# Graph attention layer on one core: who copies h in the node stage, the spacing of that stage's steps, and where the later chunks' indices stand

## The chip, the cores and the metric

The kernel runs on 1 core of one Trainium2 chip. The metric is device microseconds of one execution, lower is better. The kernel before takes 5714.75 us in the median of 3 runs (5710.31 to 5733.31).

## What is computed

One graph attention layer with a residual, over 12,500 nodes of 128 features and 412,500 edges sorted by their target:

```python
h  = relu(layernorm(x))                                   # 12500 x 128
hh, q, k, v = h @ Wn + bn, h @ Wq + bq, h @ Wk + bk, h @ Wv + bv
eh = edge_features @ We + be                              # 412500 x 128
hmid   = leaky_relu(concat(q[src], k[tgt], eh) @ A1 + b1, 0.2)
scores = leaky_relu(hmid @ A2 + b2, 0.2)                  # 8 heads
w   = softmax(scores.mean(-1), axis=0)                    # over all edges
out = segment_sum(w[:, None] * v[tgt], src)
y   = hh + out
x + gamma * (y - mean(y)) / sqrt(var(y) + eps) + beta
```

The edges arrive sorted by target, and the sum goes by source, so every edge has to be moved once.

## The kernel before

**Tiles and chunks.** Nodes are padded to 98 tiles of 128, edges to 403 groups of 8 tiles. The groups are cut into 11 chunks; the first has 57 groups (456 tiles), the next three 43 each. Each chunk goes through two stages.

**First stage** (`first_stage`). A step makes two edge tiles: four matmuls fill one PSUM bank with key and value parts (L1007 from the edge features, L1010 from a window of the node table `kv_tab`, picked by a one-hot matrix that VectorE makes at L984). One step later ScalarE copies the bank to a ring of 20 rows (L994, and L991 for the row's place), and GpSimd scatters the two tiles by indirect DMA to their sources' blocks in a table in HBM (L924). A group is four such steps, so chunk 0 has 228 of them.

**Second stage** (`second_stage`). It reads a chunk's part of the table back (L1038), computes scores and weights, and adds weighted values per node. It can begin with a chunk only when that chunk's scatters have landed.

**What must stand beside chunk 0.** In chunk 0 no second stage runs yet. Four other jobs are laid among its first-stage steps:

- `nodes` computes the node tables. A block of 4 node tiles takes 28 steps; 25 blocks follow one another, each in a software pipeline. Layer norm: `centre` (L673 to L675, VectorE), `square` (L680, ScalarE), `spread` (L685 and L687, VectorE), `root` (L690, ScalarE), `scale` (L695 and L696, VectorE). Then `turn` transposes on TensorE (L702) and `relu` evicts (L707, ScalarE). Per node tile `project` makes h, q, k and v in one PSUM bank `mp` (L714, L716). h is copied out by `keep_h` (L719). The other three are split into three bfloat16 parts, so that bfloat16 matmuls keep their precision: `upper` rounds (L722, ScalarE), `lower` subtracts (L726, VectorE), `middle` rounds the rest (L729, ScalarE), `lowest` subtracts again (L732, VectorE). `store` issues seven DMAs per block: three of `kv_tab` on SyncE's queue (L738), one of `hn_tab` (L741) and three of `q_tab` (L743) on ScalarE's queue.
- `ready(0)` and `ready(1)` give every edge of chunks 0 and 1 its slot in the table ("numbering"): a one-hot matrix on VectorE (L572), two matmuls (L579), a maximum on VectorE (L635), and after every 40 tiles a row of small VectorE operations (L593 to L619).
- `index(k)` turns the raw indices of chunk k into places, blocks and window offsets: two loads on SyncE's queue (L354, L355), thirteen VectorE operations (L359 to L392), a matmul (L371) and transposes (L398), ScalarE copies (L403, L407) and DMAs on ScalarE's queue (L381, L404, L408).
- `clear_ends` writes zeros to the table's ends (L232, SyncE).

**What sets the order.** Each engine runs its instructions in the order in which they were written out here. `interleave` deals out one step at a time of the job that is furthest behind in its share, so jobs are mixed evenly and end together. `nodes` instead is drawn by a rule inside `first_stage`: about 3.2 of its steps for each step of the first stage. Inside `nodes`, `at(t, order, job)` writes each job into a table of steps; the number is the step, counted from the block's own start t or from a node tile's start u = t + 7j. In the interleave of chunk 0 the index and numbering work is one single chain: `index(1)`, then all of `ready(1)`, then `index(2)` to `index(10)`.

Where two engines read one PSUM bank, the recording layer puts the one behind the other: `keep_h` on VectorE waits for `upper` on ScalarE, since both read `mp`.

Of the kernel before, what the change touches and what calls it, by code (L numbers as in the profile page):

```python
# [16 lines left out]
AF = mybir.ActivationFunctionType  # L17
# [48 lines left out]
NB = 4  # L66
# [3 lines left out]
LEAD = 4  # L70
# [5 lines left out]
def _ceil(a, b):  # L76
    return -(-a // b)


def interleave(*jobs):  # L80

    jobs = [[g, max(n, 1), 0] for g, n in jobs]
    while jobs:
        job = min(jobs, key=lambda j: (j[2] + 0.5) / j[1])
        try:
            next(job[0])
            job[2] += 1
        except StopIteration:
            jobs.remove(job)


def some_steps(job, n):
# [29 lines left out]
def kernel(ctx: ExitStack, tc: tile.TileContext, n_edges, x, src, dst, ea, w_nv, w_qt, w_kt,  # L122
# [12 lines left out]
    nc = tc.nc  # L135
    NP = x.shape[0]
    NTN = NP // P
# [13 lines left out]
    NC = len(chunks)  # L151
# [259 lines left out]
    def index_steps(c):  # L411
        return 12 + 2 * _ceil(chunks[c][1] * SUPER, QUAD * P)
# [228 lines left out]
    def ready(c):  # L641

        yield from count(c)
        yield from plan(c)
        yield from place_slots(c)

    def ready_steps(c):
        nt = chunks[c][1] * SUPER
        return _ceil(nt, (8 if c == 0 else 5) * STR) + 4 + 2 * _ceil(nt, STR)
# [10 lines left out]
    def nodes():  # L660
# [55 lines left out]
            nc.tensor.matmul(flat, lhsT=once3, rhs=bias3, start=False, stop=True, skip_group_check=True)  # L716

        def keep_h(b, j):
            nc.vector.tensor_copy(hns[b][:, j, :], mp[b, j][:, 0, :])  # L719

        def upper(b, j):
            nc.scalar.activation(partss[b][:, j, 0, :], mp[b, j][:, 1:4, :].rearrange("p a d -> p (a d)"), AF.Copy)  # L722
# [25 lines left out]
        def at(t, order, job, *args):  # L748
            when.setdefault(t, []).append((order, len(when.get(t, ())), job, args))

        for b in size:

            t = 28 * b
            at(t - 52, 9, load, b)
            for k, job in enumerate((centre, square, spread, root, scale)):
                at(t - 16 + 2 * k, 8, job, b)
            at(t - 5, 0, turn, b)
            at(t - 3, 0, relu, b)
            for j in range(size[b]):
                u = t + 7 * j  # L760
                at(u, 3, project, b, j)
                at(u + 3, 4, upper, b, j)
                at(u + 4, 5, keep_h, b, j)
                at(u + 5, 5, lower, b, j)
                at(u + 7, 4, middle, b, j)
                at(u + 9, 5, lowest, b, j)
            at(t + 35, 7, store, b)
        for t in range(min(when), max(when) + 1):
            for _, _, job, args in sorted(when.get(t, []), key=lambda j: j[:2]):
                job(*args)  # L770
            yield

    stored = [0]
    node_at = [0, 28 * _ceil(NTN, NB) + 35 - 2 * LEAD]


    acc = ctx.enter_context(tc.tile_pool(name="acc", bufs=1)).tile([P, NTN, D], FP, name="acc")
# [490 lines left out]
    for i, w in enumerate(units):  # L1268
        t = 2 * w["start"] - (19 if w["nq"] > 2 else 17)
# [143 lines left out]
    for c in range(NC + 1):  # L1413
        jobs = []
        if c == NC:
            count_left()
        elif c == 0:
            with tc.manual_schedule(engines={ET.PE, ET.DVE, ET.Activation, ET.SP}):
                next(first)
        if c < NC:  # L1420
            jobs.append((some_steps(first, chunks[c][1] * halves + (c == NC - 1)), chunks[c][1] * halves))
        if c > 0:
            n = ends[c] - ends[c - 1]
            idle = LEAD if c == 1 else 0
            if c == NC:
                jobs.append((fetch_early(), early + 2))
            jobs.append((chain(some_steps(second, n - 8), any_left(), some_steps(second, 8)) if c == NC else
                         chain(iter([None] * idle), some_steps(second, n - idle)), n))
        if c == 0:
            jobs.append((first_ready, (ready_steps(0) - ready_enough()) * 6 // 5))  # L1430
            jobs.append((chain(index(1), ready(1), *(index(k) for k in range(2, NC))),
                         ready_steps(1) + sum(index_steps(k) for k in range(1, NC))))
        elif c + 1 < NC:
            jobs.append((ready(c + 1), ready_steps(c + 1)))
        if c == 0:
            jobs.append((chain(*(clear_ends(k) for k in range(1, TABS))), (TABS - 1) * NTN))
        if c == 0:
            with tc.manual_schedule(engines={ET.PE, ET.DVE, ET.Activation, ET.SP}):
                interleave(*jobs)
                for _ in node_steps:  # L1440
                    pass
            setup.close()
            pb = main.enter_context(tc.tile_pool(name="pb", bufs=1))
            ps = main.enter_context(tc.tile_pool(name="ps", bufs=5))
            pq = main.enter_context(tc.tile_pool(name="pq", bufs=4))
            pw = main.enter_context(tc.tile_pool(name="pw", bufs=8))
            p3 = main.enter_context(tc.tile_pool(name="p3", bufs=1))
            ps_h = main.enter_context(tc.tile_pool(name="ps_h", bufs=2, space=PSUM))
            ps_s = main.enter_context(tc.tile_pool(name="ps_s", bufs=1, space=PSUM))
            ps_o = main.enter_context(tc.tile_pool(name="ps_o", bufs=1, space=PSUM))  # L1450
        else:
            with tc.manual_schedule(engines={ET.PE, ET.DVE, ET.Activation, ET.SP}):
                interleave(*jobs)
        if c < TABS:
            clear_holes(c)
# [90 lines left out]
```

## Time and profile before

| what | value |
|---|---|
| median of 3 runs | 5714.75 us |
| the profiled execution: its own time | 5704.97 us |
| its span, first to last instruction | 5703.2 us |
| TensorE / VectorE / ScalarE / GpSimd busy over the span | 77% / 71% / 33% / 57% |
| granted TensorE clock, mean | 0.879 |
| chunk 0: first scatter starts, last scatter ends | 72.1 us, 811.2 us |
| `keep_h`: copies, mean each | 98, 286 ns |

The span of the profiled execution is 1.8 us under its time, and its time 9.8 us under the median of the runs. PE is TensorE, DVE VectorE, ACT ScalarE, POOL GpSimd, SP SyncE; PEld is a weight load, and a q behind an engine's name is its sequencer. In a row of a group stand line, engine, operation, output and input, the count, then busy time in us and the mean of one in ns, then the engine's idle time just ahead of it and what ended it.

### The profile page before, as it was taken

What the parts mean: (1) busy time and instruction counts of PE and PEld (TensorE: products, weight loads), DVE (VectorE), ACT (ScalarE), POOL (GpSimd) and SP (SyncE); (2) the same over time, 40 slices, a digit from 0 to 9 for tenths busy, and PEclk for the clock granted to TensorE, in tenths of its full rate; (3) what the DMA queues carried; (4) which work ended last, traced back from release to release, by engine and by line L of the source; (5) the groups of instructions that cost most, each with busy time, mean ns of one, the idle gap of its engine ahead of it and who ended that gap; (6) DMA issues with size and microseconds to landing.
All of it is one profiled execution on the core that took longest, in us unless ns stands there. A gap on an engine that the chain in (4) does not pass through costs nothing. (4 is left out here: it accounts for less than half of the span.)

```text
span 5703.2 us, 86990 instructions
## 1 busy us (share of the span) xinstructions
PE 4378.4 (77%) x26559; PEld 3030.7 (53%) x26559; DVE 4076.2 (71%) x12996; ACT 1897.7 (33%) x5104; POOL 3239.9 (57%) x3250
## 2 busy tenths in 40 slices
PE   6766647877777777777777877778777787778898
PEld 3333324555555555555555555555555555556674
DVE  7777526776777666667776767777777776667898
ACT  2333322333333333333333333333333333333346
POOL 3666566665566555665655655665655665665510
PEclk8888768998898888888888988888989888989999
DMA  4667767777777777776777767777776776778985
GB/s 134 202 196 218 212 208 226 243 246 224 226 241 234 224 225 241 236 234 222 239 227 232 244 224 239 231 242 232 245 236 215 247 237 210 253 236 273 304 280 198
DMA packets 711378, 1316.75 MB, mean 231 GB/s; under 512 B 152208, under 2 KB 362309, under 8 KB 710889
## 3 DMA queue, kind: packets, MB, share of 16 engines
q1 hardware_dynamic: 492080, 867.97, 52.1%
q0 software_dynamic: 154704, 424.26, 20.1%
q10 hardware_dynamic: 64105, 18.76, 1.4%
q8 instruction: 214, 3.51, 0.3%
q14 instruction: 275, 2.25, 0.1%
HBM read 820.50 MB, written 490.10 MB: 230 GB/s over the span
## 5 line engine op out<-in xcount | busy, mean ns | idle before, releaser
L924 POOL DMA_INDIRECT tab<-row,slots x3223 | 3236.7, 1004 | 2211.9 <-ACT row L994 979.8
L1192 PE MATMUL o_ps<-rows_of,w 128*128 128x128 f32 x6860 | 1020.7, 292 | 313.4 <-DVE w L1179 170.0
L1192 PEld LDWEIGHTS o_ps<-rows_of,w 128*128 128x128 f32 x6860 | 913.5, 201 | 440.3 <-issue 258.8
L994 ACT ACTIVATE row<-row_ps 128x512 f32<-128x512 f32 x1151 | 681.2, 593 | 1126.1 <-PE row_ps L1010 343.4
L1102 ACT ACTIVATE low<-h_ps 128x512 f32<-128x512 f32 (+1 forms) x861 | 511.8, 594 | 1438.6 <-remote 432.6
L1007 PE MATMUL row_ps<-w_ea,ea_t 128*128 128x256 f32 x2302 | 821.6, 442 | 188.0 <-ACT row L994 127.0
L1179 DVE TENSOR_SCALAR w<-iota_f,rows_of,score 128x128 f32<-128x128 f32 x3381 | 954.6, 357 | 0.1
L1103 DVE TENSOR_TENSOR rows_of<-h_ps,low 128x512 f32<-128x512 f32 (+1 forms) x861 | 589.1, 684 | 497.5 <-ACT low L1102 335.0
L1093 PE MATMUL h_ps<-sel_q,qw 128*128 128x128 fp8e4 (+3 forms) x4242 | 766.9, 314 | 5.4 <-issue 5.2
L1007 PEld LDWEIGHTS row_ps<-w_ea,ea_t 128*128 128x128 f32 x2302 | 425.8, 214 | 420.9 <-issue 186.3
L1110 PE MATMUL s_ps<-rows_of,a_sb 128*32 128x384 f32 (+2 forms) x2392 | 314.7, 604 | 384.4 <-DVE rows_of L1103 257.2
L1088 PE MATMUL h_ps<-ident,rows_of 128*128 128x128 f32 x3430 | 580.1, 295 | 5.8 <-issue 5.8
L1010 PEld LDWEIGHTS <-sel 126*128 126x128 fp8e4 x3224 | 344.2, 107 | 298.4 <-issue 77.7
L1088 PEld LDWEIGHTS h_ps<-ident,rows_of 128*128 128x128 f32 x3430 | 455.1, 154 | 83.0 <-issue 44.4
L1010 PE MATMUL row_ps<-kv,sel 126*128 126x256 bf16 x2302 | 489.1, 296 | 7.0 <-issue 4.6
L1093 PEld LDWEIGHTS <-qw 128*128 128x128 bf16 x4242 | 412.5, 104 | 134.7 <-issue 39.8
L635 DVE TENSOR_REDUCE num<-run 128x5 f32<-128x490 f32 (+1 forms) x648 | 425.9, 657 | 6.4 <-PE run L579 2.2
L994 ACT ACTIVATE row<-t_bank 128x512 f32<-128x512 f32 x461 | 273.5, 593 | 465.9 <-PE t_bank L1010 190.6
L579 PE MATMUL run<-one,rest_b 128*128 128x500 f16 x637 | 263.1, 413 | 210.8 <-DVE num L635 127.9
L984 DVE TENSOR_SCALAR sel<-offs,third 126x512 fp8e4<-126x512 uint8 x806 | 365.4, 494 | 64.9 <-remote 31.8
L1078 DVE TENSOR_SCALAR sel_q<-pls,part 128x512 fp8e4<-128x512 uint8 (+1 forms) x837 | 367.7, 492 | 0.0
L1148 DVE TENSOR_SCALAR_CACHE_REDUCE s_ps<-s_ps,less_of 128x128 f32<-128x128 f32 x298 | 105.9, 355 | 365.6 <-PE o_ps L1192 114.7
(249 smaller groups left out, 4420.3 us busy)
## 6 DMA issues: line engine op xcount, KB each, us to landing
rows_of<-tab SPq DMA_DIRECT2D x264, 1542.0 KB
ea_t<-in_ea SPq DMA_DIRECT2D x403, 256.0 KB
qw<-q_tab SPq DMA_DIRECT2D x192, 384.0 KB
tab<-row,slots POOLq DMA_INDIRECT x3223
offs<-off_d SPq DMA_DIRECT2D x403, 126.0 KB
pls<-pl_d SPq DMA_DIRECT2D x264, 192.0 KB
rows_of<-tab SPq DMA_DIRECT2D x27, 1028.0 KB
qw<-q_tab SPq DMA_DIRECT2D x96, 288.0 KB
```

The lines of the kernel that those rows point to most:

```text
L635: nc.vector.tensor_reduce(num, strips[:, :NTN, :m].rearrange("p b m -> p m b"), AX.X, ALU.max)
L924: i = nc.gpsimd.indirect_dma_start(out=tab[:, :], out_offset=bass.IndirectOffsetOnAxis(ap=slots[c][t // (8 * STR)][:m, t % (8 * STR):t % ( ...
L994: nc.scalar.activation(row[:, :, 1:ROW], bank, AF.Copy)
L1007: nc.tensor.matmul(bank[:, :, 0:D], lhsT=ea_g[:, ts(k, P)], rhs=w_ea, start=True, stop=False, skip_group_check=True)
L1010: nc.tensor.matmul(bank[:, b, :], lhsT=sel[:, ts(b * halves + k, P)], rhs=kv, start=False, stop=True, skip_group_check=True)
L1078: nc.vector.tensor_scalar(sel[:, a:b], plss[i][:, a:b], part1, None, op0=ALU.is_equal, saturate=False)
L1088: nc.tensor.matmul(h_ps[:, ts(j, P)], lhsT=rows_of[i][:, a + j, 1:D + 1], rhs=ident, is_transpose=True, start=j == 0, stop=False, skip_gro ...
L1093: nc.tensor.matmul(h_ps[:, (x0 - a) * P:(x1 - a) * P], lhsT=qws[i][:, s, ts(k, D)], rhs=plss[i][:, x0 * P:x1 * P], start=False, stop=k == ...
L1102: nc.scalar.activation(low, h_ps, AF.Copy, scale=SLOPE)
L1103: nc.vector.tensor_max(rows_of[i][:, a:b, 1:D + 1], h_ps.rearrange("p (j e) -> p j e", j=m), low.rearrange("p (j e) -> p j e", j=m))
L1179: nc.vector.tensor_scalar(w, iota_f, rows_of[i][:, t, 0:1], state["score", i][:, t:t + 1], op0=ALU.is_equal, op1=ALU.mult)
L1192: nc.tensor.matmul(state["o_ps"][:, ts(t // ct, D)], lhsT=w, rhs=rows_of[i][:, t, D + 1:ROW], start=t == 0, stop=t % ct == ct - 1, skip_gr ...
```

## The change

Three things:

1. `keep_h` is an ACTIVATE on ScalarE instead of a copy on VectorE.
2. Inside `nodes` the distances grow. Layer norm: `centre` starts 20 steps ahead of the block instead of 16, and the links then stand 2, 3, 4 and 3 steps apart instead of 2 each; `scale` stays 8 ahead. Split: `keep_h` stays at u+4, `lower` goes from u+5 to u+6, `middle` from u+7 to u+10, `lowest` from u+9 to u+13. `store` goes from t+35 to t+36.
3. `index(2)` to `index(10)` no longer follow `ready(1)`; a new `mixed` (the body of `interleave` as a generator) deals them out evenly beside it.

```diff
-def interleave(*jobs):
+def mixed(*jobs):
...
             jobs.remove(job)
+            continue
+        yield
+
+def interleave(*jobs):
+    for _ in mixed(*jobs):
+        pass
...
         def keep_h(b, j):
-            nc.vector.tensor_copy(hns[b][:, j, :], mp[b, j][:, 0, :])
+            nc.scalar.activation(hns[b][:, j, :], mp[b, j][:, 0, :], AF.Copy)
...
-            for k, job in enumerate((centre, square, spread, root, scale)):
-                at(t - 16 + 2 * k, 8, job, b)
+            for before, job in ((20, centre), (18, square), (15, spread), (11, root), (8, scale)):
+                at(t - before, 8, job, b)
...
                 at(u + 3, 4, upper, b, j)
-                at(u + 4, 5, keep_h, b, j)
-                at(u + 5, 5, lower, b, j)
-                at(u + 7, 4, middle, b, j)
-                at(u + 9, 5, lowest, b, j)
-            at(t + 35, 7, store, b)
+                at(u + 4, 4, keep_h, b, j)
+                at(u + 6, 5, lower, b, j)
+                at(u + 10, 4, middle, b, j)
+                at(u + 13, 5, lowest, b, j)
+            at(t + 36, 7, store, b)
...
-    node_at = [0, 28 * _ceil(NTN, NB) + 35 - 2 * LEAD]
+    node_at = [0, 28 * _ceil(NTN, NB) + 36 - 2 * LEAD]
...
-            jobs.append((chain(index(1), ready(1), *(index(k) for k in range(2, NC))),
-                         ready_steps(1) + sum(index_steps(k) for k in range(1, NC))))
+            others = sum(index_steps(k) for k in range(2, NC))
+            jobs.append((chain(index(1), mixed((ready(1), ready_steps(1)), (chain(*(index(k) for k in range(2, NC))), others))),
+                         index_steps(1) + ready_steps(1) + others))
```

Line numbers in the changed kernel are higher by 8 from `some_steps` on: L719 becomes L727, L726 L734, and so on.

VectorE's queue at group 16 of chunk 0, from that group's one-hot matrix (`sel`) on, kernel before. `hn`, `rest` and `parts` are the node stage's, `one` and `num` the numbering's:

```order
L984 TENSOR_SCALAR sel<-offs,third 126x512 x2
L719 COPY hn<-mp 128x128
L726 TENSOR_TENSOR rest<-mp,parts 128x384
L572 TENSOR_TENSOR one<-bins_b,near 128x500
L635 TENSOR_REDUCE num<-run 128x5
L732 TENSOR_TENSOR parts<-rest,parts 128x384
L719 COPY hn<-mp 128x128
L726 TENSOR_TENSOR rest<-mp,parts 128x384
L572 TENSOR_TENSOR one<-bins_b,near 128x500
L635 TENSOR_REDUCE num<-run 128x5
```

The same group of the changed kernel; `f`, `head` and `base` belong to the index of chunk 4:

```order
L992 TENSOR_SCALAR sel<-offs,third 126x512 x2
L740 TENSOR_TENSOR parts<-rest,parts 128x384
L734 TENSOR_TENSOR rest<-mp,parts 128x384
L373 SCALAR_TENSOR_TENSOR f<-whole,raw_src 128x264
L580 TENSOR_TENSOR one<-bins_b,near 128x500
L643 TENSOR_REDUCE num<-run 128x5
L376 TENSOR_TENSOR head<-raw_dst,bound 1x33
L378 CAST base_i<-head 1x33
L740 TENSOR_TENSOR parts<-rest,parts 128x384
L734 TENSOR_TENSOR rest<-mp,parts 128x384
```

The copy of h is gone from VectorE. The subtraction `rest` of one node tile now stands directly behind the subtraction `parts` of the tile before it. Index steps stand between the steps of the numbering, where before the index of chunk 2 came only after the whole numbering of chunk 1; by this place the queue held 58 numbering steps before and holds 44 now.

ScalarE's queue around the seventh store, kernel before (`row` is the eviction to the ring):

```order
L722 ACTIVATE parts<-mp 128x384
L991 ACTIVATE row<-place_228 128x4
L994 ACTIVATE row<-row_ps 128x2x256
L729 ACTIVATE parts<-rest 128x384
L741 DMA hn_tab<-hn 128x4x128
L743 DMA q_tab<-parts 128x4x128 x3
L994 ACTIVATE row<-row_ps 128x2x256
L722 ACTIVATE parts<-mp 128x384
```

And around the seventh store of the changed kernel (`sq_n` is layer norm's square):

```order
L999 ACTIVATE row<-place_228 128x4
L1002 ACTIVATE row<-row_ps 128x2x256
L749 DMA hn_tab<-hn 128x4x128
L751 DMA q_tab<-parts 128x4x128 x3
L1002 ACTIVATE row<-row_ps 128x2x256
L737 ACTIVATE parts<-rest 128x384
L730 ACTIVATE parts<-mp 128x384
L688 ACTIVATE sq_n<-xt 128x512
L727 ACTIVATE hn<-mp 128x128
```

The rounding of one tile's rest (L737) now stands directly ahead of the next tile's `upper` (L730), and the copy of h follows that, here with a square between the two. The four DMA issues of the store stay where they were among the evictions.

## Prediction

> **What bounds the kernel now.** All edits lie in the work beside chunk 0, so I first asked how long that stretch is and who is full in it. The table by stage, cut at the first scatter (72 us), at 500 and 740 us and at chunk 0's last scatter (811 us), with one later chunk for comparison:
>
> ```profile
> core 0 of [0], span 5703.2 us
> core 0: us, PE busy (x) PEld busy (x) DVE busy (x) ACT busy (x) POOL busy (x), PEclk, DMA share, GB/s
> 72.00:500.00 428.00, 307.97 (x1126) 153.56 (x1125) 336.59 (x939) 156.43 (x373) 274.18 (x268) 0.82 0.71 203
> 500.00:740.00 240.00, 150.33 (x481) 73.83 (x480) 136.15 (x388) 84.11 (x205) 138.05 (x140) 0.75 0.75 209
> 740.00:811.00 71.00, 32.30 (x110) 18.54 (x109) 12.25 (x39) 15.24 (x37) 48.14 (x50) 0.67 0.65 189
> 1376.00:1949.00 573.00, 449.46 (x2713) 312.43 (x2712) 418.20 (x1343) 183.99 (x488) 347.24 (x345) 0.90 0.77 233
> 72.00:811.00 739.00, 490.60 (x1714) 245.93 (x1712) 484.99 (x1365) 255.78 (x615) 460.37 (x456) 0.78 0.72 204
> ```
>
> Nobody is full, but the load is uneven. VectorE is 79% busy up to 500 us (336.59 of 428), 57% up to 740 and 17% in the tail, although GpSimd's scatters ask for the same work in every step. The scatters, in the group view of the 739 us:
>
> ```profile
> L924 POOL DMA_INDIRECT tab<-row,slots x456 | 460.6, 1010 | 346.8 <-ACT row L994 207.1 <-issue 127.3 <-ACT off_t L403 5.2
> POOL tab L924 <- ACT row L994: 207.1, 55, 68.3
> ```
>
> The second row is from the waits: 68.3 us of the 207.1 is the wait for the first scatter. So GpSimd, in its own pace of scatter and issue, was held up for 346.8 - 68.3 - 127.3 = 151 us. That is the ceiling of any gain here: chunk 0 can't be through in less than 739 - 151 = 588 us. What it wins reaches the end, since the second stage's first load comes right behind the last scatter of chunk 0 (timeline, GpSimd and SyncE's queue):
>
> ```profile
> 810.28 0.97 POOL L924 DMA_INDIRECT tab<-row,slots  x1 [0.30 <-issue]
> 825.56 0.39 SPq L1038 DMA_DIRECT2D rows_of<-tab  x1
> ```
>
> From there on nothing is changed, so I let the remaining 4,892 us shift as a block.
>
> **The copy of h.** What its line waited for in the whole run and, in the waits, the longest (10.3 us), and VectorE's groups in the 739 us:
>
> ```profile
>   ACT parts L722: 53.2, 20
>   issue: 43.4, 16
> DVE hn L719 <- ACT parts L722: 52.6, 18, 10.3
> L635 DVE TENSOR_REDUCE num<-run 128x5 f32<-128x490 f32 x152 | 99.7, 657 | 3.3 <-PE row_ps L1010 2.1 <-remote 0.9 <-PE run L579 0.3
> L572 DVE TENSOR_TENSOR one<-bins_b,near 128x500 f16<-128x500 bf16 (+2 forms) x151 | 70.2, 465 | 22.0 <-PE mp L716 5.2 <-remote 5.0 <-PE run L579 3.9
> L732 DVE TENSOR_TENSOR parts<-rest,parts 128x384 bf16<-128x384 f32 x93 | 51.1, 550 | 21.9 <-ACT parts L729 12.0 <-issue 4.4 <-ACT row L991 2.0
> L726 DVE TENSOR_TENSOR rest<-mp,parts 128x384 f32<-128x384 f32 x93 | 50.9, 547 | 0.0
> L719 DVE COPY hn<-mp 128x128 f32<-128x128 f32 x92 | 26.4, 287 | 97.0 <-ACT parts L722 52.6 <-issue 43.4 <-ACT row L994 0.8
> ```
>
> VectorE loses 92 copies, 26.4 us. The copy is also where VectorE stands idle longest, 97.0 us, because it waits for `upper` one step behind it; numbering, one-hot matrices and layer norm queue behind that. On ScalarE no copy of 128x128 out of PSUM is in the trace. The nearest rows:
>
> ```profile
> L994 ACT ACTIVATE row<-row_ps 128x512 f32<-128x512 f32 x227 | 134.3, 593 | 219.6 <-issue 57.7 <-PE row_ps L1010 52.8 <-remote 39.2
> L403 ACT ACTIVATE off_t<-t_bank 128x256 uint8<-128x256 f32 (+1 forms) x10 | 3.7, 375 | 15.9 <-DMA hn_tab<-hn 7.0 <-DMA q_tab<-parts 6.4 <-PE t_bank L398 2.5
> L407 ACT ACTIVATE off_t<-t_bank 8x128 uint8<-8x128 f32 (+2 forms) x10 | 2.7, 269 | 9.8 <-issue 2.5 <-DMA q_tab<-parts 2.3 <-DMA tab<-blank 2.3
> ```
>
> It costs 269 ns (128 columns) to 375 ns (mostly 256), so 98 copies add 26 to 37 us to ScalarE; I take 27, as the width is the lower row's. ScalarE is busy 255.78 of 739 us, and I cost the addition at nothing, because 219.6 us of its idle time lies ahead of evictions alone. Where that cover is gone, an eviction is late by one copy, 0.27 us.
>
> **The wait that stays.** `lower` reads the bank that the copy has just left, so it now waits for ScalarE's copy in place of VectorE's own. It stands at u+6 where the wait stood at u+4. A step lasts 739 / (228 x 3.19) = 1.02 us (228 first-stage steps, 727 / 228 = 3.19 node steps in each). Two steps are 2.03 us, less 0.28 for the copy ahead: 1.75 us of slack for each of the 36 waits of the line view, 63 us at most. Short waits can't give 1.75, so I take 48 of the 97 us as gone and 49 as left, now at `lower`. The Trainium skill, "PSUM — Partial Sum Buffer", section "PSUM bank collisions raise a hardware error", has the rule for it: two engines may not touch one bank at once, not even both reading, so an order between them must stand. The trace agrees: the copy, which needs nothing of `upper`, was released by it. By that rule alone the wait moves and keeps its length, and the time would be the second rival's, 5,688.
>
> `middle` to `lowest` goes from two steps to three, `lower` to `middle` from two to four. Their waits, 21.9 us at L732 and ScalarE's 30.9 us for `rest` (its waits are quoted next), should mostly go: 2 us or more of slack against waits of about 1.5 us in the mean. That buffers come free later costs nothing: there are two each of `rest` and `mp`, the tile two on writes its `rest` at u+20, after `lowest` at u+13, and its `mp` at u+14, after `lower` at u+6. Layer norm's links are nearly free as well, 14.6 us at the root.
>
> ```profile
> ACT parts L729 <- DVE rest L726: 30.9, 20, 5.9
> ACT rstd_n L690 <- DVE rstd_n L687: 14.6, 6, 6.3
> ```
>
> What does not go: the store's issues hold ScalarE. One of them, in its timeline, with the next copy 6.37 us late:
>
> ```profile
> 636.24 4.88 ACTq L743 DMA_DIRECT2D q_tab<-parts  x3
> 641.16 0.38 ACT L403 ACTIVATE off_t<-t_bank 128x256 uint8<-128x256 f32 x1 [6.37 <-DMA q_tab<-parts]
> ```
>
> This comes 25 times before and after.
>
> **The indices.** Where the ten of them start (first VectorE operation, by stretch: 72 to 500, to 740, to 811), and what it waits for:
>
> ```profile
> 72.00:500.00 428.00, 0.80 (x2) 0.82 0.71 203
> 500.00:740.00 240.00, 2.11 (x7) 0.75 0.75 209
> 740.00:811.00 71.00, 0.30 (x1) 0.67 0.65 189
> L359 DVE TENSOR_SCALAR whole<-raw_src 128x264 f32<-128x264 int32 (+2 forms) x10 | 3.2, 320 | 22.1 <-DMA raw_src<-in_src 16.8 <-issue 5.4
> L371 PE MATMUL t_bank<-head,ones 1*128 1x33 f32 (+2 forms) x20 | 5.2, 348 | 28.3 <-DVE rest L726 7.4 <-DVE rstd_n L687 6.8 <-issue 6.1
> SPq L966 <- PE row_ps L1010: 81.2, 15, 10.3
> ```
>
> Eight start after 500 us, behind the whole numbering of chunk 1. The 126 steps of the nine later chunks (14 each) are 43% of a chain of 296 steps; the change lays them over 95% of it, so one comes every 0.95 x 739 / 126 = 5.6 us instead of every 2.5. All their instructions move: VectorE's thirteen, the matmul and transposes on TensorE, two loads on SyncE's queue, two copies and three DMA issues on ScalarE's, as many as before. SyncE's loads move past the first stage's loads (L966), which already wait for buffers (81.2 us), so they cost nothing there. The waits for loads and for the offset's matmul (22.1 and 28.3 us) should mostly be covered. In exchange the numbering of chunk 1, 69 steps of L572 and L635 (1.12 us each, 77 us), is stretched over the whole of chunk 0 and takes up the idle VectorE of the tail.
>
> **The sum.** These terms overlap, so I don't add them; I ask what pace the evened load allows. TensorE has 490.60 us of work in the stretch. At the share that it reaches up to 500 us, 307.97 / 428 = 0.720, this takes 682 us; at the share of the later chunk, 449.46 / 573 = 0.784, 626 us. VectorE has 485.0 - 26.4 = 458.6 us, and at its own best share, 0.786, 583 us, below GpSimd's floor of 588: it stops being the limit. I take TensorE's 0.720 by two thirds and 0.784 by one third, 0.741, because the queues and the 25 stores stay those of this stage: 490.6 / 0.741 = 662 us, 77 us less than 739. The bare stall terms (26 for the copy, 48 for its wait, 15 of the 21.9 at L732, 17 for the loads) make 106 us of VectorE's queue, so 77 asks for nothing beyond them. The profiled execution's 5,705.0 us (span 5,703.2) become 5,628; it lies 9.8 us under the median of the runs, 5,714.75, so I predict 5,638.
>
> **The rivals.**
>
> First, GpSimd becomes the bound (chance 0.12). With VectorE and TensorE evened out, ScalarE could run ahead by the ring, and stores would be hidden. Chunk 0 ends at the floor: about 140 of the 151 us, 5,575. For it: the tail from 740 us already runs near that pace. Against: TensorE would be busy 490.6 of 599 us, 0.82, which no stage here shows.
>
> Second, the wait only moves (0.17). `lower` waits as long as the copy did, ScalarE being late by stores and evictions that no distance cures; the longest was 10.3 us. Then only the copy's 26.4 us go: 5,688. Against: the mean wait is 96.6 / 36 = 2.7 us, and the new slack 1.75.
>
> Third, slower: ScalarE's queue becomes the link (0.08). It feeds GpSimd, and gets 98 copies ahead of evictions. The third `q_tab` issue needs `lowest` of the last tile, which was five steps ahead of the store (30 against 35) and is now two (34 against 36); while it waits, evictions wait. Price: 27 us of copies and one step at each store, 25 x 1.02 = 25 us, so 52, 5,767, if the spread gains nothing. It decides once GpSimd's wait for the eviction exceeds the present 207.1 us. The Trainium skill, "ScalarE: Activation LUTs", section "Rules for kernel authors", speaks for it: simple elementwise work belongs on VectorE, ScalarE being slower per element. No row here shows the two on one shape.
>
> Fourth, given back (0.04). Numbering and indices of the set-up now end with chunk 0, and the second stage's buffers take their memory. If that holds its first load, the start is no earlier: 5,715.
>
> **How the numbers follow.** The measurement can tell about 0.5% (28.6 us) from no change. My forecast, 5,638, with 5,602 to 5,658 as its own range (TensorE at 0.784 and at 0.720), has 0.59; it and the first rival are faster, 0.71. The second and fourth are within the bound, 0.21. The third is slower, 0.08. Eight in ten takes the first rival in at the low end and the second and fourth at the high end: 5,565 to 5,715.
>
> **What would show it.** Right: the last scatter of chunk 0 ends near 734 us instead of 811; index operations lie evenly between 100 and 730; VectorE's share is between 0.65 and 0.72 throughout; the idle time ahead of `rest` (L734) is about 50 us, and at `parts` (L740, L737) a few; a later chunk still takes 573 us. Wrong: as much idle time ahead of L734 as there was at L719 (second rival); more than 207 us of GpSimd waiting for evictions (third); a gap between last scatter and first load well over 15 us (fourth); or an unchanged pace in spite of shorter waits, which would mean that another queue sets it.

## The result and the profile after

| | before | after |
|---|---|---|
| median of 7 runs each, us | 5,714.75 (5,698.71 to 5,736.8) | 5,686.88 (5,675.43 to 5,691.66) |
| ratio, 95% interval | | 0.9946 [0.9926, 0.9966] |
| profiled execution, span, us | 5,704.97, 5,703.2 | 5,675.43, 5,673.7 |
| first to last scatter of chunk 0, us | 739.1 | 712.0 |

The change is faster by 28 us between the medians, 0.5%. The direction and the range were right; the forecast was 77 us, so only 36% of it came. The same kernel was met in two conditions, a long one in which the kernel before takes 5,625 to 5,715 us in the median of a series, and a short one in which it takes 4,705 to 4,717 us; the result above and the profile behind the forecast are of the long one, and every comparison of times below stays within one condition.

The table by stage of the changed kernel, with the same columns as before; the rows are all of chunk 0, its three stages, and a later chunk:

```profile
71.00:783.00 712.00, 489.14 (x1707) 246.14 (x1706) 466.16 (x1269) 266.46 (x706) 459.23 (x456) 0.78 0.75 211
72.00:500.00 428.00, 304.63 (x1103) 154.43 (x1103) 307.96 (x831) 170.13 (x454) 276.92 (x274) 0.81 0.74 213
500.00:740.00 240.00, 163.41 (x546) 80.58 (x545) 151.47 (x421) 87.08 (x230) 151.98 (x153) 0.77 0.79 216
740.00:783.00 43.00, 20.11 (x61) 11.13 (x60) 5.73 (x17) 8.44 (x20) 29.43 (x31) 0.58 0.57 167
1350.00:1914.00 564.00, 444.57 (x2724) 311.11 (x2723) 417.51 (x1346) 183.94 (x489) 347.08 (x345) 0.91 0.77 237
```

VectorE is more even (72%, 63%, 13%, against 79%, 57%, 17%). It works 466.2 us in place of 485.0, and stands idle 245.8 us in place of 254.0. In VectorE's account of the 27 us that chunk 0 became shorter, 19 are therefore work that it no longer has, and only 8 are waiting that went. TensorE's share went from 0.664 to 0.687. The last scatter of chunk 0 and the second stage's first load, from the timeline:

```profile
782.00 1.05 POOL L932 DMA_INDIRECT tab<-row,slots  x1 [0.30 <-issue]
795.41 0.40 SPq L1046 DMA_DIRECT2D rows_of<-tab  x1
```

Chunk 0 ends 28.2 us earlier (811.25 to 783.05), and the span is 29.5 us shorter: nearly all of the gain lies in chunk 0, and the rest moved with it as a block. Now the groups of chunk 0 that answer to those shown of before (lines are 8 further down in the changed code: the copy is L727, `lower` L734, `lowest` L740, the one-hot of the numbering L580, the eviction L1002, the first operation of an index L367 and the matmul of its offset L379):

```profile
L932 POOL DMA_INDIRECT tab<-row,slots x456 | 459.3, 1007 | 319.9 <-issue 130.4 <-ACT row L1002 76.0 <-DVE parts L740 67.5
L1002 ACT ACTIVATE row<-row_ps 128x512 f32<-128x512 f32 x227 | 134.1, 597 | 276.6 <-remote 98.7 <-PE row_ps L1018 74.5 <-issue 53.3
L580 DVE TENSOR_TENSOR one<-bins_b,near 128x500 f16<-128x500 bf16 x149 | 69.6, 467 | 69.5 <-remote 37.4 <-PE run L587 14.6 <-PE row_ps L1018 7.3
L734 DVE TENSOR_TENSOR rest<-mp,parts 128x384 f32<-128x384 f32 x93 | 51.3, 552 | 54.2 <-ACT hn L727 31.1 <-issue 14.4 <-PE run L587 5.1
L740 DVE TENSOR_TENSOR parts<-rest,parts 128x384 bf16<-128x384 f32 x93 | 51.3, 551 | 32.1 <-ACT parts L737 18.5 <-issue 9.3 <-ACT row L1002 4.1
L727 ACT ACTIVATE hn<-mp 128x128 f32<-128x128 f32 x92 | 25.3, 275 | 0.0
L367 DVE TENSOR_SCALAR whole<-raw_src 128x264 f32<-128x264 int32 (+2 forms) x10 | 3.0, 300 | 3.0 <-issue 2.9
L379 PE MATMUL t_bank<-head,ones 1*128 1x33 f32 (+2 forms) x20 | 4.8, 326 | 13.4 <-issue 6.5 <-DVE head L376 5.0 <-DVE f L373 1.1
```

The 97.0 us ahead of the copy are gone, and 54.2 stand ahead of `lower`. But ahead of `lowest` there are 32.1 us (21.9 before), and ahead of the numbering's one-hot 69.5 (22.0 before), most of these put down to "remote". The three places together held 140.9 us before and hold 155.8 now. GpSimd's row gives the sum of chunk 0 on its side: 459.3 of scatters, 130.4 of issue and 319.9 - 130.4 - 67.5 = 122.0 of being held up (67.5 is, all but 0.3, the wait for the first scatter, which lies ahead of the stretch) are 712. It was held up 151 us before, so 29 of the 151 were won.

"Remote" is a wait whose end the profile puts down to no instruction that it knows. These are the largest such waits in chunk 0, us in total, times and longest, of before and then of after:

```profile
ACT row L994 <- remote: 39.2, 10, 6.0
DVE sel L984 <- remote: 31.8, 3, 17.7
ACT parts L722 <- remote: 9.1, 3, 3.9
ACT hT L707 <- remote: 5.5, 5, 2.4
DVE one L572 <- remote: 5.0, 3, 2.2
```

```profile
ACT row L1002 <- remote: 98.7, 26, 7.2
DVE one L580 <- remote: 37.4, 9, 7.6
DVE sel L992 <- remote: 20.2, 2, 13.1
ACT hT L715 <- remote: 15.8, 5, 6.6
```

All such waits of chunk 0 together are 97 us before (27 waits) and 193 us after (53). Each figure is of one execution, and they differ much from one to the next: a second profile of the kernel before, among the experiments, has 128 us, and two profiles of one and the same kernel (the steps alone) have 155 and 85. So they are large enough to matter, but by how much the change made them grow is not shown; what they are is taken up below.

### The profile page after: what moved, and what is told of

It reads as the page before. It is cut to its first block, busy times and chain, and to the rows that moved or that the text cites. A ratio compares the mean times of both kernels' runs of the same rounds, so it can differ in the third digit from the quotient of the medians.

```text
span 5673.7 us, 87035 instructions
## 1 busy us (share of the span) xinstructions
PE 4379.2 (77%) x26559; PEld 3025.9 (53%) x26559; DVE 4060.5 (72%) x12898; ACT 1906.9 (34%) x5202; POOL 3237.5 (57%) x3250
## 5 line engine op out<-in xcount | busy, mean ns | idle before, releaser
L1002 ACT ACTIVATE row<-row_ps 128x512 f32<-128x512 f32 x1151 | 680.3, 594 | 1222.6 <-PE row_ps L1018 414.0
L643 DVE TENSOR_REDUCE num<-run 128x5 f32<-128x490 f32 (+1 forms) x648 | 426.1, 658 | 24.6 <-PE row_ps L1018 14.4
L1002 ACT ACTIVATE row<-t_bank 128x512 f32<-128x512 f32 x461 | 273.3, 593 | 489.5 <-PE t_bank L1018 170.2
L580 DVE TENSOR_TENSOR one<-bins_b,near 128x500 f16<-128x500 bf16 (+1 forms) x648 | 301.6, 465 | 84.0 <-remote 37.4
```

The lines of the kernel that those rows point to most:

```text
L643: nc.vector.tensor_reduce(num, strips[:, :NTN, :m].rearrange("p b m -> p m b"), AX.X, ALU.max)
L1002: nc.scalar.activation(row[:, :, 1:ROW], bank, AF.Copy)
```

## The experiments

Theory A was that the spreading of the indices brings most of the gain, theory B that the copy and the steps together do, the copy alone being worth nothing since the wait moves with it; theory C, that the two banks in which the first stage's steps are summed hold back what is left. Theory F came out of the first runs: that in the long condition TensorE's late completions (matmuls whose end is signalled some us after the profile shows them over) cover most of the gain. Theories D, E, G and H are told where an expectation names them. The us behind a ratio are worked out from it and from the median of the kernel before; for the whole change above that would be 31 us.

**The parts, in the long condition** (kernel before 5,691.32 us, 32 runs). The first kernel has only the copy:

```
-            nc.vector.tensor_copy(hns[b][:, j, :], mp[b, j][:, 0, :])
+            nc.scalar.activation(hns[b][:, j, :], mp[b, j][:, 0, :], AF.Copy)
...
```

> The kernel before with the copy of h on ScalarE and nothing else changed. Theory A (chunk 0's pace is set by TensorE's and VectorE's queues in turn, waits on ScalarE only cover for them): VectorE loses 26 us of work and the wait at the copy moves to the subtraction behind it, so some 5 to 10 us less than before (ratio about 0.9985). Theory B (what holds the stretch is ScalarE's lateness at the links of the split): the copy comes one instruction later in ScalarE's queue ahead of a subtraction only one step on, so 0 to 10 us more than before (1.000 to 1.002).

Measured 1.0001 [0.9987, 1.0015]. The second has only the steps, the copy staying on VectorE:

```
...
-                at(u + 5, 5, lower, b, j)
-                at(u + 7, 4, middle, b, j)
-                at(u + 9, 5, lowest, b, j)
-            at(t + 35, 7, store, b)
+                at(u + 6, 5, lower, b, j)
+                at(u + 10, 4, middle, b, j)
+                at(u + 13, 5, lowest, b, j)
+            at(t + 36, 7, store, b)
...
```

> The kernel before with the longer distances of layer norm, split and store alone; the copy stays on VectorE at u+4 and the indices stay behind the numbering. Theory A: the links' waits shorten but show up again at the numbering, so within 5 us of before (0.999 to 1.001). Theory B: the subtractions stop waiting for ScalarE, 15 to 25 us less (0.996 to 0.997).

Measured 0.9981 [0.9963, 0.9998], 11 us, between what the two theories expected. The third has only the mixing of the later chunks' indices with the second numbering:

```
-            jobs.append((chain(index(1), ready(1), *(index(k) for k in range(2, NC))),
...
+            jobs.append((chain(index(1), mixed((ready(1), ready_steps(1)), (chain(*(index(k) for k in range(2, NC))), others))),
...
```

> The kernel before with the later chunks' indices laid beside the second chunk's numbering and nothing else. Theory A: it evens out the load of VectorE and TensorE, and so brings most of the measured 28 us: 15 to 25 us less (0.9955 to 0.9975). Theory B: the links of the split keep their waits, under 8 us less (0.9985 to 1.000).

Measured 0.9993 [0.9976, 1.0009]. The fourth has the copy and the steps, without the mixing:

> The changed kernel with the indices put back behind the numbering: copy and distances alone. Theory A: 5 to 12 us less than before (0.998 to 0.999). Theory B: 20 to 30 us less, nearly all of the change (0.995 to 0.9965).

Measured 0.9963 [0.9945, 0.9982], 21 us. Theory A falls: the mixing alone can't be told from nothing. B holds: copy and steps bring 21 us, most of the 31 that the whole change has by its ratio in the first comparison, and the copy alone nothing.

**A third bank, and more work for each engine, in the short condition.** These four are the changed kernel with one edit each. They met the short condition (kernel before 4,705.25 us, 9 runs). First, every third step of chunk 0 takes a third bank, which is freed by letting the transposes of the node stage use `mp`'s buffers:

```
-            tpos[b] = tps.tile([P, NB, P], FP, name="tp")
+            tpos[b] = mps.tile([P, NB, P], FP, name="mp")
...
+        if c == 0 and taken[0] % 3 == 1:
+            return third_bank
```

> The changed kernel with a third PSUM bank for the first stage's steps in chunk 0 (the transposes of the node stage give up their own bank and take one of the two of the projections). Theory C (the pace is set by the round between TensorE and ScalarE over two eviction banks, with one step of slack; every stall on either passes to the other): TensorE's wait for an eviction, 124 us in chunk 0, falls by half or more and chunk 0 ends 25 to 60 us earlier than the changed kernel's, ratio to before 0.984 to 0.990. Theory D (TensorE's own matmul time is the bound): at most 10 us, 0.993 to 0.9955. Theory E (VectorE's queue, in which numbering, one-hot matrices and the split follow in strict order, is the bound): at most 10 us as well.

Measured 0.9863 [0.9846, 0.9881]. Next, the bias matmul of `project` is made twice, the first being overwritten (an estimated 42 us more for TensorE in the whole run; in chunk 0 its busy time came out 50 us longer); the last subtraction of `lowest` is made twice (98 times 551 ns, 54 us more for VectorE); the copy of h is made twice (98 times 275 ns, 27 us more for ScalarE):

```
+            nc.tensor.matmul(flat, lhsT=once3, rhs=bias3, start=True, stop=False, skip_group_check=True)
```

> The changed kernel with the bias matmul of the node projection done twice (the first time into the bank that the projection then overwrites), 98 x 0.43 = 42 us more work for TensorE and nothing else. Theory D: nearly all of it shows, 30 to 42 us over the changed kernel, ratio to before 1.000 to 1.002. Theories C and E: half or less, 10 to 20 us, 0.9965 to 0.998.

```
+            nc.vector.tensor_sub(partss[b][:, j, 2, :], rests[b, j], partss[b][:, j, 1, :])
```

> The changed kernel with the last subtraction of the split done twice, 98 x 0.55 = 54 us more work for VectorE. Theory E: nearly all of it shows, 40 to 54 us over the changed kernel, ratio to before 1.0015 to 1.004. Theories C and D: 10 to 20 us, 0.9965 to 0.998.

```
+            nc.scalar.activation(hns[b][:, j, :], mp[b, j][:, 0, :], AF.Copy)
```

> The changed kernel with the copy of h done twice on ScalarE, 98 x 0.275 = 27 us more work on its queue, ahead of evictions and of the subtraction that waits for the bank. Theory C: 10 to 20 us over the changed kernel, ratio to before 0.9965 to 0.998. Theories D and E: under 5 us, 0.9945 to 0.9955. If the third rival of the prediction has any weight, 20 us or more.

Measured 0.9893 [0.9876, 0.9911] with more for TensorE, 0.9917 [0.9902, 0.9932] with more for VectorE, 0.9863 [0.9844, 0.9882] with more for ScalarE. They mean little until the change itself is known in this condition, which the next runs give.

**The change and its parts, in the short condition** (kernel before 4,716.71 us, 11 runs). The change itself, unaltered:

> The changed kernel itself, once more, beside three others. In the runs e5 to e8 the kernel before took 4,705 us, not 5,691 as in e1 to e4, so the two groups can't be compared over the ratio of the change. Theory F (in the slower condition TensorE's completions come late by some us a couple of hundred times in a run, and that covered most of the change's gain): where the kernel before takes about 4,700 us the change gives a ratio of 0.984 to 0.989, and where it takes about 5,700 us 0.993 to 0.996. Theory G (the gain is the same 0.5% whatever the condition, and the third bank, the doubled copy and the rest gained by themselves): 0.993 to 0.996 in either.

Measured **0.9861 [0.9842, 0.9881]**, 66 us: within theory F's span, and theory G falls. That the late completions are the reason is not shown by this alone, as the section on the prediction says. The third bank, again beside it:

> The third bank of e5, beside the changed kernel under one condition. Theory C (two eviction banks with one step of slack set the pace of chunk 0): 0.4% or more below e9. Theory F with VectorE, GpSimd and the ring of rows as the limits: within 0.2% of e9 in the fast condition; in the slow one, where completions come late, a step more of slack takes 10 us or more off, 0.2 to 0.5% below e9.

Measured 0.9870 [0.9849, 0.9891], the same as without it: theory C falls. A small worth isn't ruled out: in both profiles with the third bank chunk 0 takes 607 us from first to last scatter, where the change takes 617, though the time of the whole run doesn't show it. The mixing alone, and copy with steps:

> The indices beside the second chunk's numbering alone, beside the changed kernel under one condition. Theory F in the fast condition: evening out the load is worth 20 us or more where TensorE isn't late, 0.992 to 0.996; in the slow one as in e3, 0.998 to 1.001. Theory G: 0.998 to 1.001 in either.

> Copy and distances alone, beside the changed kernel under one condition. Theory F in the fast condition: about half of the change, 0.991 to 0.995; in the slow one as in e4, 0.9945 to 0.998. Theory G: 0.9945 to 0.998 in either.

Measured 0.9939 [0.9918, 0.9959], 29 us, and 0.9887 [0.9866, 0.9908], 53 us. In this condition the mixing is worth something too, and the two do not add (82 against 66). Copy and steps bring four fifths of the change here, where theory F had expected about half.

Against the change itself (0.9861) the doubled work of the runs above reads so, with about 12 us of uncertainty on each: TensorE's 42 us cost 15, VectorE's 54 us cost 26, ScalarE's 27 us cost 1. So VectorE and TensorE share the bound, each showing only a part of its added work, and no cost of ScalarE's can be told from nothing. How full the two got, in chunk 0 of the kernel with more for TensorE, and of the one with more for VectorE:

```profile
73.00:698.00 625.00, 506.41 (x1869) 246.16 (x1870) 472.92 (x1300) 270.35 (x717) 461.81 (x456) 0.84 0.84 241
```

```profile
77.00:704.00 627.00, 461.95 (x1779) 241.12 (x1778) 522.07 (x1396) 270.56 (x717) 467.53 (x456) 0.84 0.84 241
```

TensorE reaches 0.81 of its stretch in the one, VectorE 0.83 in the other, each with more work in a stretch of 625 and 627 us against 617 of the change. The share that TensorE or VectorE had in the change (0.74 and 0.77) was therefore no ceiling.

**Once more before, copy and steps.** Three more kernels, with expectations for the short condition, met the long one (kernel before 5,624.96 us, 23 runs):

> The kernel before itself, for its profile in the fast condition (ratio 0.998 to 1.002). Theory F: chunk 0's last scatter ends 35 us or more after that of e9 (677 us there or thereabouts), none of its waits is put down to a releaser that the profile doesn't know, VectorE's idle time ahead of the copy of h is above 50 us, and all later chunks last as long as those of e9 within 3 us each. Theory G: chunk 0 differs from e9 by no more than the 28 us of the first comparison.

> The copy on ScalarE alone, in the fast condition. Theory F: VectorE's 26 us of work are gone, but the subtraction stays one step behind: half of it, 0.996 to 0.999. Rival H (the copy alone has no worth, as in e1): 0.999 to 1.001.

> The longer distances alone, in the fast condition. Theory F: they carry most of what copy and distances bring together (0.9887), 0.990 to 0.994. Rival H (the distances need the copy to be gone from VectorE): 0.996 to 0.999.

Measured 0.9990 [0.9976, 1.0004] for the kernel before against itself, so that 0.1% means nothing here; 0.9989 [0.9973, 1.0004] for the copy, which can't be told from that; 0.9943 [0.9927, 0.9960], 32 us, for the steps. The steps' worth differs between the two times that it was measured in this condition (11 and 32 us), and so do the waits without a known releaser in the two profiles (155 and 85 us in chunk 0). Three more met the short condition (kernel before 4,710.56 us, 18 runs):

> The kernel before itself. It would settle what the kernel before looks like where TensorE's completions come in time. Theory F (late completions covered most of the gain where the change was measured): if the run falls where the same kernel takes some 4,710 us, VectorE and ScalarE have no wait over 0.8 us that the profile puts down to nothing it knows, and chunk 0's first scatter to its last takes 616.7 us of the changed kernel plus some 60, about 680 us. Rival (the changed kernel gains elsewhere): chunk 0 takes the changed kernel's 616.7 us within 20, and the 66 us lie in the later chunks. Where it falls in the other condition, about 739 us again and nothing is told apart.

> The steps between the links alone, without the copy on ScalarE and without the index spreading. If the run falls where the kernel takes some 4,710 us: theory B (the steps bring most, the copy alone nothing) has 25 to 45 us, ratio 0.990 to 0.995, of the 54 us that copy and steps had together there. Rival (the copy frees VectorE, and where completions come in time VectorE's work is the bound, so that the copy brings as much alone): under 20 us, 0.996 or more. In the other condition 11 to 26 us as measured.

> The copy of h on ScalarE alone. If the run falls where the kernel takes some 4,710 us: theory B has nothing, ratio 0.998 to 1.001, since what VectorE no longer works it waits at the next link. Rival (VectorE's work is the bound there): 26 us less work of VectorE is worth 15 to 26 us, 0.9945 to 0.997. In the other condition nothing, as twice before.

Measured 1.0000 [0.9989, 1.0011] for the kernel before, whose chunk 0 takes 675 us (theory F had about 680), 0.9906 [0.9890, 0.9921], 44 us, for the steps, and 0.9969 [0.9958, 0.9979], 15 us, for the copy. The last is at the edge of the rival's span and outside theory B's: where completions come in time, the 26 us of work that leave VectorE are worth somewhat over half of themselves (the wait that moves with the copy grows by 12 us, as shown below), and "the copy alone brings nothing" holds in the long condition only.

Now the kernel before and the change can be laid side by side in the short condition. Chunk 0 from its first scatter to its last, and GpSimd's group there, of the kernel before:

```profile
72.00:747.00 675.00, 477.79 (x1778) 247.48 (x1777) 490.46 (x1395) 261.16 (x626) 463.90 (x456) 0.81 0.78 224
L924 POOL DMA_INDIRECT tab<-row,slots x456 | 463.9, 1017 | 279.1 <-ACT row L994 158.1 <-issue 106.0 <-DMA tab<-row,slots 3.4
```

and of the changed kernel:

```profile
71.00:688.00 617.00, 456.75 (x1780) 238.42 (x1779) 472.21 (x1301) 269.57 (x718) 463.37 (x456) 0.84 0.87 244
L932 POOL DMA_INDIRECT tab<-row,slots x456 | 463.6, 1017 | 220.8 <-issue 103.3 <-DVE parts L740 67.6 <-ACT row L1002 16.2
```

The stretch is 58 us shorter (the span 67), where it became 27 us shorter in the long condition. VectorE works 18 us less, as there, but its idle time falls by 40 us (184.5 to 144.8), where it fell by 8. GpSimd was held up 279.1 - 106.0 - 68.1 = 105 us before (68.1 is the wait for the first scatter) and 220.8 - 103.3 - 67.6 = 50 after: the 55 us between them are nearly all of the 58.

The chain of copy and subtractions in the waits, first of the kernel before, then with the copy alone (its group row of `lower`), then of the whole change:

```profile
DVE hn L719 <- ACT parts L722: 81.1, 33, 10.5
ACT parts L729 <- DVE rest L726: 79.3, 48, 7.3
ACT rstd_n L690 <- DVE rstd_n L687: 30.8, 14, 5.5
DVE parts L732 <- ACT parts L729: 13.4, 9, 4.4
```

```profile
L726 DVE TENSOR_TENSOR rest<-mp,parts 128x384 f32<-128x384 f32 x93 | 51.3, 552 | 93.2 <-ACT hn L719 93.2
```

```profile
DVE parts L740 <- ACT parts L737: 33.9, 13, 6.9
ACT parts L737 <- DVE rest L734: 31.2, 22, 5.2
DVE rest L734 <- ACT hn L727: 25.9, 25, 4.9
```

This is the change's mechanism in one view. The copy by itself only moves the wait: 81.1 us ahead of the copy become 93.2 ahead of `lower`. The longer distances then take it down to 25.9, and ScalarE's wait for `rest` from 79.3 to 31.2. Not all of that is won. 20 us come back ahead of `lowest`, and ahead of `middle` ScalarE is idle for 73.3 us in place of 79.8, because 31 us are now put down to the store's DMA issues on its queue, and none were before.

The same waits with the steps alone, the copy still on VectorE:

```profile
ACT parts L737 <- DVE rest L734: 56.3, 28, 7.7
DVE hn L727 <- ACT parts L730: 48.2, 23, 7.6
DVE parts L740 <- ACT parts L737: 4.4, 1, 4.4
```

Here the copy stands one step behind `upper`, as it always did, and yet its wait fell from 81.1 to 48.2 us. So the slack at one link is not the whole story: with the longer distances ScalarE comes less late to that link too. Its wait at layer norm's root, 30.8 us before, is gone in this run, which fits. The steps alone bring 44 of the 66 us.

## Why the prediction was right and wrong

**Where the time lies and how it reaches the end**: right. 28.2 of 29.5 us lie in chunk 0, and the rest moved as a block. A later chunk took 564 us and not 573; that was given back within the other chunks, since the rest of the span changed by 1.3 us in all.

**The copy**: right in its price. The 92 copies in the stretch took 25.3 us on ScalarE, 275 ns each, which makes 27 us for all 98, as forecast. They cost nothing there that can be measured: 27 us more in the same place cost 1 us, with about 12 us of uncertainty. The Trainium skill, "ScalarE: Activation LUTs", section "Rules for kernel authors", would have simple operations such as `add` and `mul` on VectorE, and its reason is a speed per element that it gives for bf16. This copy reads and writes float32, and the trace has 275 ns for it on ScalarE against 287 on VectorE. So the reason doesn't reach this case, and it falls as grounds for the third rival.

**The wait that stays**: right in size, 48 of 97 us forecast to go, 43 gone, 54 left, at `lower`, but partly by luck. Of the 97 us the row of the copy puts only 52.6 down to `upper` and 43.4 to "issue", time in which VectorE waited for nothing that the profile shows; the prediction took both as waits for `upper`. After, 31.1 are put down to the copy and 14.4 to "issue", so more of the second kind went than of the first, and the slack of two steps was not worked out for those. The order that the rule of the Trainium skill asks for ("PSUM — Partial Sum Buffer", section "PSUM bank collisions raise a hardware error": two engines may not touch one bank at once) is put in by the recording layer, and no run here tests the rule itself. What such an order does is seen with the copy alone, where the wait moved at more than its full length (81.1 to 93.2); the longer distances are what shortened it. Wrong beside it: the waits at `lowest` and `middle` were to shrink to a few us. Ahead of `middle` ScalarE's wait for `rest` shrank only from 30.9 to 9.7. Ahead of `lowest` the idle time grew, 21.9 to 32.1, and the wait 13.4 to 33.9 in the short condition, in spite of one more step. With the steps alone it did shrink, to 4.4; it is the copy on ScalarE beside the steps that moves the lateness one link on (26.7 with both and without the mixing).

**The indices**: half right. The idle time ahead of their first operation fell from 22.1 us to 3.0 (L367), and that ahead of the offset's matmul from 28.3 to 13.4 (L379). They are spread, but too early: eight of the ten start before 500 us, and the last at 628. The tail was not filled: VectorE has 5.73 of 43 us there, since numbering and node work end before 740 us, and the last 31 scatters run near GpSimd's pace (29.43 of 43 us busy, and mostly 0.30 of issue ahead of each). Cut at the same 740 us, the tail is 43 us long and not 71 only because it ends earlier.

**The sum**: the step that failed. "I take TensorE's 0.720 by two thirds and 0.784 by one third, 0.741": that made 662 us of chunk 0, and it took 712, at a share of 0.687. Two things were wrong with it.

First, it took 77 of TensorE's 248 us of idle time (739 - 490.6) as waiting for links that the change would ease. Only 26 of them went (712 - 489.1 leaves 223). Its check on VectorE's queue failed in the same way: of 80 us of waits that it named there (48, 15 and 17), VectorE's idle time fell by 8, since what went at the copy and at the loads came back elsewhere, 47.5 us of it ahead of the numbering's one-hot. In the long condition part of the idle time doesn't belong to these links at all. The timeline of the changed kernel at one such place (start, duration, engine, line, idle time ahead and what ended it):

```profile
227.94 0.70 PE L1015 MATMUL row_ps<-w_ea,ea_t 128*128 128x256 f32 x2
227.99 2.93 ACTq L751 DMA_DIRECT2D q_tab<-parts  x3
228.48 0.39 PE L1018 MATMUL row_ps<-kv,sel 126*128 126x256 bf16 x2
229.03 0.96 POOL L932 DMA_INDIRECT tab<-row,slots  x1 [0.30 <-issue]
230.29 0.96 POOL L932 DMA_INDIRECT tab<-row,slots  x1 [0.30 <-issue]
233.31 0.60 ACT L1002 ACTIVATE row<-row_ps 128x512 f32<-128x512 f32 x1 [5.42 <-remote]
233.40 0.47 DVE L580 TENSOR_TENSOR one<-bins_b,near 128x500 f16<-128x500 bf16 x1 [5.95 <-remote]
233.97 1.22 PE L1015 MATMUL row_ps<-w_ea,ea_t 128*128 128x256 f32 x2 [5.10 <-ACT row L1002]
```

By the profile, which models the ends of matmuls, the bank's last matmul is over at 228.87 and ScalarE's issues at 230.92, yet ScalarE's eviction of that bank starts at 233.31, and VectorE's next instruction, which waits for TensorE as well, starts with it. The trace's semaphore events agree: TensorE's signals stop at 228.27 us and come again from 232.53 on. VectorE and TensorE have no instruction at all in these 4.4 us, ScalarE only the issues, and TensorE ends up waiting for ScalarE. The engines in this gap, in the columns of the table by stage:

```profile
228.87:233.31 4.44, 0.00 (x0) 0.00 (x0) 0.00 (x0) 0.00 (x0) 1.92 (x2) 1.00 1.09 319
```

TensorE's clock was granted in full (1.00), so no matmul was slowed by the clock then. Nor is it one that the record lost: every profile has the same 26,559 matmuls (and 26,657 where the bias matmul is made twice). Neither instruction waits for a link of the split, so a longer distance between links can't help here. Ahead of the numbering's one-hot such waits were 5.0 us before and 37.4 after, ahead of the evictions 39.2 and 98.7; but the first is also 27.5 without the mixing and 22.0 with the mixing alone, each in one execution, so no part of the change can be named for it. The comparison of the two conditions fits: 28 us where these waits are, 66 us where the trace has none. Not shown is that they alone make the difference. TensorE's granted clock in chunk 0 differs too, 0.78 before and after in the long condition, 0.81 and then 0.84 in the short one; the 21 us by which TensorE's busy time falls there would be worth about 7 by the price of the doubled matmul (15 us for 42).

Second, the method was wrong even where its number comes out. In the short condition TensorE's share after the change is 456.75 / 617 = 0.740, what was forecast, and the time came 1.4% down, as forecast (5,638 of 5,714.75 is 1.3%). That is luck: with one more matmul in each node tile the share became 0.81, which the prediction had held against its first rival as shown by no stage. A share of busy time follows from the work and the pace; it didn't set the pace here.

**The rivals.** The first (GpSimd's floor) was not reached: 122 of its 151 us are left, and 50 of 105 in the short condition. The second named 5,688 us and the time is 5,687, but its mechanism is not what happened: the wait shortened by 43 us. What it described, the copy alone, is worth 0 to 15 us. The third (ScalarE's queue) is ruled out by GpSimd's waits for evictions, which were to exceed 207.1 us and fell to 76.0 (169 with 25.0 for the rows' places and the 67.5 of the first scatter), and in the short condition by the doubled copy. The fourth (given back at the second stage's start) is ruled out by the gap between the last scatter's start and the first load, 13.4 us against 15.3 before.

## What to carry to other kernels

When an operation on a bank moves to another engine, look for the next instruction that must wait for that bank: the wait goes there whole, and more distance along the whole chain of links, not only at that one, is what shortens it. An engine's share of busy time in one stage is no limit that another mix of work can be priced by; count instead how long the engine that sets the end is held up (here GpSimd, 151 us), and ask who releases it each time. Before pricing waits as if they would go, sort out those that the profile puts down to nothing it knows: in this case no run of the long condition was without them, and they hold whichever instruction waits next.

## What the runs showed of the hardware

The kernel before takes 5,625 to 5,715 us or 4,705 to 4,717 us, for a whole series of runs at a time. In the long condition ScalarE and VectorE wait some 270 times in a run for a signal that comes when by the profile the matmuls are over. The two largest such rows of the whole run, kernel before:

```profile
ACT low L1102 <- remote: 432.6, 100, 9.6
ACT row L994 <- remote: 310.1, 106, 13.5
```

They make 743 us, and the spans differ by 988 (5,703.2 against 4,715.5). In the short condition the waits have no such row in any of the eleven profiles. The mean granted clock was 0.88 to 0.89 in the one and 0.93 to 0.94 in the other; TensorE's busy time is 352 us longer in the long one (4,378.4 against 4,026.5), so the two hundred-odd late signals are not all of the difference. The number of the chip doesn't decide it: the record lists chip 7 for a short series (4,716.71 us) and for a long one (5,624.96 us). What delays these completions, and whether the lower mean clock is its cause or its result, stays open: no run here could set the condition. A gain measured in one of them is not the gain in the other (0.9946 and 0.9861 for the same change), so a change that is worth half a per cent should be read within one condition and, where possible, in both.
